# Gathering the keys of AUGRU steps 4 to 11 as 32x32 blocks

## The chip, the core and the metric

The kernel runs on one core of a Trainium2 chip. The time is the device time of one execution in microseconds, the median of several. A core has five engines that run beside each other and wait for one another by semaphores: PE (matrix multiply), DVE (vector), ACT (activations), POOL (here: elementwise work and gathers) and SP (here: issuing DMAs). Data between HBM and the on-chip memory is moved by 16 DMA engines, which serve the queues of SP, ACT and POOL. A gather is an indirect DMA that POOL issues: 128 rows, each from an address that an index gives.

## The reference

1024 users have a history of 100 items with 128 features. The reference runs a GRU over the history, scores each of its states with a small attention network, takes a softmax over the steps, and then runs a second recurrent network, AUGRU, over the same GRU states ("keys"), whose update gate is scaled by an attention weight. A state is picked at each user's own length, and a small network gives one score per user.

```python
    r = sigmoid(i_r + h_r); z = sigmoid(i_z + h_z)       # GRU, 100 steps
    n = tanh(i_n + r * h_n)
    h_new = (1.0 - z) * n + z * h                        # = keys[:, t]
...
attn = softmax(where(mask == 1, score, -inf), axis=1)[..., 0]
pooled = einsum('bt,btd->bd', attn, keys)
att_seq = pooled.T[:T]
...
    r = sigmoid(ti @ aug_Wr.T + aug_br)                  # AUGRU, 100 steps; ti = [h, keys_t]
    u = sigmoid(ti @ aug_Wu.T + aug_bu)
    h_hat = tanh(concatenate([h * r, x_t]) @ aug_Wh.T + aug_bh)
    u = a_t[:, None] * u
    h_new = (1.0 - u) * h + u * h_hat
```

The weight `a_t` of AUGRU step t is row t of the pooled keys, transposed. So AUGRU can't begin its second product before the softmax and the pooling of all 100 steps are done.

## The kernel before, in words

The 1024 users are two halves of 512 columns; a state is a 128 x 512 tile with features in partitions. All numbers are 32-bit floats. The order of the instructions on each engine is the order in which the program writes them (there is no scheduler in between).

**GRU phase** (`gru_phase`, L180). In each of 100 steps, for each half, PE does six 128x512 products (L501; two matmul instructions each in the profile), ACT and DVE the gates, and the attention network of the step before follows (L663). POOL keeps a masked sum of the history and the weighted sum of the keys, `pooled` (L580 to L600). After each step DVE transposes the new state in 32x32 blocks (`transpose`, L540, DVE L550) into a tile `kt` that holds G = 4 steps, and SP writes it to HBM, to `keys_d[q]`, for AUGRU. There are two layouts:

- Groups q below `WHOLE` = 2, that is steps 0 to 3 and 4 to 7, are stored as whole rows: one row per user with four steps of 128 features. Each step of a half costs four DMAs of 64 KB (L556).
- Later groups hold eight steps and are stored as blocks: partition p of `kt` as it stands, in one DMA of 1 MB per half and four steps (`store`, L562, L564).

**The hand-over.** AUGRU takes the users sorted by length, so that later steps are narrower (`WIDTHS`, 512 columns at step 0, 496 at step 4, 96 from step 83 on). Keys are therefore read back by gathers through sorted indices (`load_rows`, L153). A group of whole rows takes 4 gathers per half, of 256 KB each (`gather`, L142 to L144). A group of blocks takes one gather for 32 users, 16 for a half, each of 128 rows of 1 KB (L168); in the AUGRU phase a tiny POOL copy in front of each (L167) reads one column of `rest`, a tile that the current half-step just wrote, so that gathers are spread over the half-steps ("pace").

Rows of group 0 are gathered in the last 30 GRU steps. Those of group 1, half 0, in step T-2, those of half 1 right after the loop (L867, L885). Behind the loop come the last softmax blocks, the rest of the pooling (POOL L589 to L600 for half 0, DVE for half 1), the write of `pooled_d` (L941, L1208) and eight gathers `att_r` of it (`gather_weights`, L987); PE turns them into the weights of steps 0 and 1 (L996).

**AUGRU phase** (`augru_phase`, L943). A half-step (`half_step`, L1069) closes the two gates of step t of one half on PE (L1058: pr, pu), then opens the three gates of the next half-step from its key (`open_gates`, L1049, L1054: pr, ph, pu); the product ph with the reset state follows in the next half-step. ACT does two sigmoids and a tanh; DVE the five products L1082, L1084, L1086, L1092 and L1095, where L1095 writes `rest`, a tile of a pool with three buffers. SP loads the attention weights two steps ahead (L1027).

`load_key` (L1032) makes the key tile two steps ahead, in the half-step of step t - 2. From whole rows that is four PE transposes into a PSUM bank (L1040) and an ACT copy (L1041). From blocks it is one DVE block transpose (L1044), since a 32x32 block needs only to be turned in itself.

Which gathers stand in which half-step is planned by `spread` (L1192): the gathers of group q begin when group q - 1 becomes current and end three or four steps before group q is needed. Gathers go into `kp`, a pool of four buffers; `kx`, a pool of two buffers of half that size, holds `kt` tiles in the GRU phase and the early rows at its end.

Of the kernel before, what the change touches and what calls it, by code (L numbers as in the profile page):

```python
# [9 lines left out]
F32 = mybir.dt.float32  # L10
# [9 lines left out]
P = 128  # L20
B = 1024
T = 100
HB = 512
NH = B // HB
NG = B // P
GH = HB // P

R = 32
KH = HB // R
# [20 lines left out]


G = 4
WHOLE = 2
READ = [G] * WHOLE + [2 * G] * ((T - WHOLE * G) // (2 * G))
READ += [T - sum(READ)] * (sum(READ) < T)
FIRST = [sum(READ[:q]) for q in range(len(READ))]
# [22 lines left out]
def kernel(ctx: ExitStack, tc: tile.TileContext, a: dict, out: bass.AP):  # L79
# [26 lines left out]
    nc = tc.nc  # L106
# [32 lines left out]
    kx = ctx.enter_context(tc.tile_pool(name="kx", bufs=NH))  # L139
    later = {}  # L140
# [10 lines left out]
    rows = {}  # L151

    def load_rows(q, i, width, tiles):  # L153

        n = READ[q]
        if q < WHOLE:
            tag = "kt" if q else "once"
            r = rows[q, i] = tiles.tile([P, GH, n * P], F32, tag=tag, name="rows")
            for g in range(GH):
                gather(r[:, g, :], keys_d[q], g, i)  # L160
                yield
            return
        r = rows[q, i] = tiles.tile([P, KH, n * R], F32, tag="rows", name="rows")
        for k in range(-(-width // R)):
            if later.get("pace") is not None:

                nc.gpsimd.tensor_copy(r[:, k, 0:1], later["pace"])  # L167
            nc.gpsimd.indirect_dma_start(  # L168
                out=r[:, k, :],
                out_offset=None,  # L170
                in_=keys_d[q],
                in_offset=bass.IndirectOffsetOnAxis(ap=idx_k[:, k, i : i + 1], axis=0),
            )
            yield

    def all_of(steps):
        for _ in steps:
            pass

    def gru_phase(pools):  # L180
# [34 lines left out]
        kp = pools.enter_context(tc.tile_pool(name="kp", bufs=3 * NH))  # L215
# [578 lines left out]
        def stage(count=1):  # L794
            for _ in range(count):
                if soft["stages"]:
                    soft["stages"].pop(0)()
# [8 lines left out]

        rest = load_later()
        early = [load_rows(0, i, HB, mid) for i in range(NH)]
        more_early = [load_rows(1, i, HB, kx) for i in range(NH)]

        late, again, early_from = 6, 24, 84
        for s in range(T):
            last = s == T - 1
            n, due = divmod(s - again, 4)
            n, i = divmod(n, NH)
            more_history = 0 <= n < late

            def loads():
                for half in halves:
                    for m in range(1, AHEAD + 1) if s == 0 else (AHEAD,):  # L820
                        if s + m < T:
                            half.load(s + m)
                            if s + m >= late:
                                half.load_mask(s + m)
                    if s == T - AHEAD:
                        half.load_features()
                if more_history and due == 0:
                    halves[i].load(n, again=True)
                    halves[i].load_mask(n)

            def after_gate():
                if s:
                    take(s - 2)
                    for half in halves:
                        half.product(s - 1)
                loads()

            staged = None
            for half in halves:
                half.gru(  # L840
                    s,
                    after_gate if half.i == 0 else nothing,
                    (lambda: half.transpose(s - 1)) if s else nothing,
                )
                if half.i == 0:
                    staged = bool(soft["stages"])
                    stage(0 if last else 1)
            exponents()
            if s == 0:
                attention_weights()  # L850
            else:
                if not staged:
                    next(rest, None)
                if s == 1:
                    item_part()
                attend(s - 1)

            for n_x in range(s + (s > early_from), min(s + (s >= early_from), T - 1) + 1):
                for half in halves:
                    if n_x >= late:  # L860
                        half.history(n_x)
            for half in halves:
                if last:
                    half.cross_features()

            if s == T - 2:
                all_of(more_early[0])  # L867
            for half in halves:
                half.pool(2 if len(half.todo) > 7 or s >= 92 else 1, nc.gpsimd)
                if s >= GATHER:  # L870
                    next(early[half.i], None)
            if more_history and due == 2:
                halves[i].history(n)
# [8 lines left out]
            for f in these:  # L882
                next(features[f])

        all_of(more_early[1])  # L885
        take(T - 2)
        for half in halves:
            half.product(T - 1)
# [12 lines left out]
        n = ENDS[-3] - ENDS[-4] + 1  # L901
# [19 lines left out]
            half.store((T - 1) // G)  # L921
        halves[1].pool(T, nc.vector)
        stage()
        halves[0].pool(T, nc.gpsimd)
        some(5, 6)
        some(7)
# [3 lines left out]
        stage()  # L930
        halves[0].pool(T, nc.gpsimd)
        halves[1].pool(T, nc.vector)


        for half in reversed(halves):
            t = blocked(s_bs[NH * (soft["j"] % 2) + half.i])
# [6 lines left out]
    def augru_phase(pools, widths, alive):  # L943
# [7 lines left out]
        kp = pools.enter_context(tc.tile_pool(name="kp3", bufs=4))  # L951
# [35 lines left out]
        def gather_weights(i):  # L987
            r = wp.tile([P, GH, P], F32, name="att_r", bufs=2)
            for g in range(GH):
                gather(r[:, g, :], pooled_d, g, i)  # L990
            return r
# [40 lines left out]
        def load_key(t, i, n=None):  # L1032

            q = max(j for j, first in enumerate(FIRST) if first <= t)
            w, m, r = widths[t], t - FIRST[q], rows[q, i]
            k = qp.tile([P, HB], F32, name="k3")
            if q < WHOLE:
                p = pa.tile([P, HB], F32, tag="a", name="pk3") if n is None else bank("pk3", n)
                for g in range(-(-w // P)):
                    nc.tensor.transpose(p[:, ts(g, P)], r[:, g, ts(m, P)], ident)  # L1040
                nc.scalar.copy(k[:, :w], p[:, :w])  # L1041
            else:
                w = -(-w // R)
                nc.vector.transpose(  # L1044
                    k.rearrange("p (k r) -> p k r", r=R)[:, :w, :], r[:, :w, ts(m, R)]
                )
            keys[t, i] = k

        def open_gates(t, i, banks=(None,) * 3):  # L1049
# [19 lines left out]
        def half_step(t, i):  # L1069


            w, h = widths[t], h3[i][:, : widths[t]]
            before, after = ((t - 1, 1), (t, 1)) if i == 0 else ((t, 0), (t + 1, 0))
            if before in resets:
                open_state(*before)
            pr = close_gate(t, i, "pr", wr, h)
            pu = close_gate(t, i, "pu", wu, h)
            nc.scalar.activation(pr, pr, AF.Sigmoid, bias=later["br"])
            nc.scalar.activation(pu, pu, AF.Sigmoid, bias=later["bu"])
            state = states.pop(1 - i, None)  # L1080
            if state is not None:
                nc.vector.tensor_mul(state[0], state[0], state[1])  # L1082
            r = wp.tile([P, HB], F32, name="r3")[:, :w]
            nc.vector.tensor_mul(r, h, pr)  # L1084
            if state is not None:
                nc.vector.tensor_sub(state[3], state[0], state[2])  # L1086
            if t == 1 and i == 0:
                store_weights(0, pa.tile([P, HB], F32, tag="a", name="pw"))
                first_state(1, spare)
            elif t == 1:  # L1090
                first_weights(1, spare)
            nc.vector.tensor_mul(pu, pu, att.pop((t, i))[:, :w])  # L1092
            rest = wp.tile([P, HB], F32, name="rest")[:, :w]

            nc.vector.scalar_tensor_tensor(  # L1095
                out=rest, in0=pu, scalar=1.0, in1=h, op0=ALU.subtract, op1=ALU.mult
            )
            later["pace"] = rest[:, 0:1]
            resets[t, i] = r, pu, rest
            if after[0] < T and (*after, "pr") not in opened:  # L1100
                open_gates(*after)
            if t == 1 and i:
                store_weights(1, spare)
            if t + 2 < T:
                load_att(t + 2, i)
            if 1 < t < T - 2:
                load_key(t + 2, i)

        def last_state(i):
# [97 lines left out]
        for to, t in later["att", 0][: G - 1]:  # L1207
            nc.scalar.dma_start(out=to, in_=t)  # L1208
        sorted_rows = [gather_weights(i) for i in range(NH)]
        for i in range(NH):  # L1210
            load_key(2, i, (FREE_BANK, None)[i])
        open_gates(1, 1, EARLY_BANKS)
# [118 lines left out]
```

## Time and profile before

| | us |
|---|---|
| median of 10 runs | 2058.49 (2057.82 to 2060.6) |
| the profiled execution, and its span | 2058.26, 2056.4 |
| GRU loop on PE | 4.1 to 1412.7 |
| hand-over, to the first AUGRU half-step that closes gates | 1412.7 to 1462.5 |
| AUGRU steps 1 to 99 and the last network | 1462.5 to 2056 |

The profile is one execution, recorded instruction by instruction. A line of the order of time gives the start and the length in microseconds, the engine, the line of the kernel, the operation, the tiles (out<-in) with shapes, and in brackets how long the engine had been idle and what ended that. "x4" merges neighbours of one kind. A line of a stretch gives, for a window of time, the busy time of each engine with its number of instructions, the granted clock of PE as a share of full speed, the busy share of the DMA engines and GB/s. A line of a group gives busy time, mean length in ns, and idle time in front. Matmuls are pipelined and their ends are modelled, so PE's starts say more than its lengths.

### The profile page before, as it was taken

Reading aid. Unit: us, or ns where it says so; the run is one execution under the profiler, and the core shown is the slowest. Engines: PE = TensorE matmul, PEld = TensorE weight load, DVE = VectorE, ACT = ScalarE, POOL = GpSimd, SP = SyncE. Lnnn points to the kernel's source line nnn. Section 1 sums busy time; section 2 is a strip of 40 time slices with the busy share of each in tenths; the row PEclk is TensorE's granted clock in tenths of the full one; section 3 lists DMA queues with packets and bytes.
Section 4 is the critical chain, followed back from the end, with each engine's and each line's share of the span. In section 5 each row is a group of like instructions: output and inputs, shape, how many; then the busy total and the mean of one; then the engine's idle time right before and its main releaser. Section 6 shows DMA issues by size and latency. Waiting matters only on the chain. (4 is left out here: it accounts for less than half of the span.)

```text
span 2056.4 us, 26797 instructions
## 1 busy us (share of the span) xinstructions
PE 2027.5 (99%) x8320; PEld 979.4 (48%) x8320; DVE 1748.4 (85%) x3050; ACT 831.3 (40%) x1516; POOL 1305.0 (63%) x1299
## 2 busy tenths in 40 slices
PE   8999999999999999999999999999899999999997
PEld 3343343333333333333333333334444556679997
DVE  6888999998989988989889898999567787888886
ACT  3334343343433343433333333343344444445554
POOL 0333939669796959596896868898645434444332
PEclk9999999999999999999999999999999999999999
DMA  4643333323334333333333323323434333333332
GB/s 118 118 94 89 104 103 97 92 81 98 111 105 105 117 104 118 111 103 102 98 103 99 104 90 102 104 88 104 119 103 112 96 91 99 92 98 100 87 77 36
DMA packets 254132, 204.36 MB, mean 99 GB/s; under 512 B 76006, under 2 KB 217034, under 8 KB 253978
## 3 DMA queue, kind: packets, MB, share of 16 engines
q1 hardware_dynamic: 240266, 170.43, 30.0%
q0 software_dynamic: 12128, 31.91, 5.5%
q8 instruction: 68, 1.11, 0.2%
q14 instruction: 86, 0.70, 0.1%
q10 hardware_dynamic: 1584, 0.20, 0.1%
HBM read 146.43 MB, written 54.40 MB: 98 GB/s over the span
## 5 line engine op out<-in xcount | busy, mean ns | idle before, releaser
L501 PE MATMUL ps<-x,wih 128*128 128x512 f32 x1200 | 592.7, 603 | 4.1 <-DMA x<-in_hist_x 4.1
L501 PE MATMUL ps<-hn,whh 128*128 128x512 f32 x1188 | 574.4, 592 | 0.0
L501 PEld LDWEIGHTS ps<-x,wih 128*128 128x128 f32 x1200 | 220.9, 191 | 327.7 <-issue 257.6
L501 PEld LDWEIGHTS ps<-hn,whh 128*128 128x128 f32 x1188 | 225.7, 190 | 284.1 <-issue 274.6
L487 POOL TENSOR_TENSOR xm<-x,m 128x512 f32<-128x512 f32 x200 | 248.2, 1241 | 135.2 <-DMA m<-mask_d 134.8
L532 ACT ACTIVATE ps<-ps,bih 128x512 f32<-128x512 f32 x200 | 132.4, 662 | 476.1 <-DVE ps L531 476.1
L513 ACT ACTIVATE r<-ps,brz 128x512 f32<-128x512 f32 x200 | 137.5, 687 | 384.6 <-PE ps L501 384.0
L488 POOL TENSOR_TENSOR hist<-hist,xm 128x512 f32<-128x512 f32 x200 | 268.8, 1344 | 15.7
L600 POOL TENSOR_TENSOR pooled<-pooled,kw 128x512 f32<-128x512 f32 x191 | 254.0, 1330 | 15.0
L599 POOL TENSOR_TENSOR kw<-kt,e 128x512 f32<-128x512 f32 x191 | 220.0, 1152 | 64.7 <-DVE e L772 64.6
L168 POOL DMA_INDIRECT rows<-keys_d,idx_k x204 | 199.0, 975 | 82.1 <-POOL rows L167 50.2
L576 DVE TENSOR_TENSOR kq<-hn,item 128x512 f32<-128x512 f32 x200 | 224.4, 1161 | 0.0
L663 PE MATMUL pm<-hn,wk 128*32 128x512 f32 x1200 | 211.6, 596 | 3.2 <-ACT q L242 1.7
L663 PE MATMUL pm<-kq,wkq 128*32 128x512 f32 x1200 | 209.2, 592 | 0.0
L1066 ACT ACTIVATE c<-ph,bh 128x96 f32<-128x96 f32 (+41 forms) x198 | 96.5, 487 | 257.2 <-PE ph L1058 228.9
L663 PE MATMUL pm<-mv,w 128*32 128x512 f32 (+1 forms) x808 | 195.8, 598 | 0.7 <-DVE e L753 0.7
L697 DVE TENSOR_TENSOR f<-pm,q 128x512 f32<-128x512 f32 x200 | 128.4, 684 | 53.5 <-PE pm L663 53.4
L167 POOL COPY rows<-rest 128x1 f32<-128x1 f32 x204 | 38.7, 190 | 202.7 <-DVE rest L1095 198.8
L536 DVE TENSOR_TENSOR d<-hn,ps 128x512 f32<-128x512 f32 x198 | 136.1, 687 | 34.8 <-ACT ps L532 32.5
L1082 DVE TENSOR_TENSOR pu<-pu,c 128x96 f32<-128x96 f32 (+41 forms) x197 | 88.3, 448 | 89.3 <-ACT c L1066 80.8
L537 DVE TENSOR_TENSOR d<-ps,d 128x512 f32<-128x512 f32 x200 | 138.4, 692 | 23.7 <-ACT ps L533 6.9
L531 DVE TENSOR_TENSOR ps<-ps,u 128x512 f32<-128x512 f32 x200 | 140.0, 700 | 21.5 <-PE ps L501 0.5
(180 smaller groups left out, 3019.6 us busy)
## 6 DMA issues: line engine op xcount, KB each, us to landing
x<-in_hist_x SPq DMA_DIRECT2D x212, 256.0 KB
keys_d<-kt SPq DMA_DIRECT2D x46, 1024.0 KB
m<-mask_d SPq DMA_DIRECT2D x200, 128.0 KB
keys_d<-kt SPq DMA_DIRECT2D x64, 64.0 KB
rows<-keys_d,idx_k POOLq DMA_INDIRECT x204
s_b<-mv SPq DMA_DIRECT2D x200, 8.0 KB
at<-att_d SPq DMA_DIRECT2D x34, 48.0 KB
mask_i<-in_mask SPq DMA_DIRECT2D x8, 200.0 KB
```

What stands on the lines that cost most here:

```text
L168: nc.gpsimd.indirect_dma_start(out=r[:, k, :], out_offset=None, in_=keys_d[q], in_offset=bass.IndirectOffsetOnAxis(ap=idx_k[:, k, i : i + ...
L487: nc.gpsimd.tensor_mul(d, x, m)
L488: nc.gpsimd.tensor_add(acc, acc, d)
L501: nc.tensor.matmul(p, lhsT=w[:, g, :], rhs=v, start=(j == 0), stop=(j == len(parts) - 1),)
L513: nc.scalar.activation(r, pr, AF.Sigmoid, bias=brz[:, 0:1])
L531: nc.vector.tensor_add(pi, pi, u)
L536: nc.vector.tensor_sub(d, h, pi)
L537: nc.vector.tensor_mul(d, pz, d)
L576: nc.vector.tensor_mul(kq, h, item[:, self.cols])
L599: eng.tensor_mul(d, k, w)
L600: eng.tensor_add(acc, acc, d)
L663: nc.tensor.matmul(p[i][s, :], lhsT=w[:, s], rhs=v, start=start, stop=stop)
```

## The change

`WHOLE` goes from 2 to 1. Group 0 (steps 0 to 3) stays in whole rows; all others are blocks of eight steps, 4 to 11, 12 to 19 and so on to 92 to 99, where they were 8 to 15 and so on with four steps left at the end. So:

- In GRU steps 4 to 7 the 32 small stores become two of 1 MB.
- Half 0 of the new group 1 is gathered by the end of the GRU phase into two `kx` tiles of 8 blocks each: 4 gathers in step T-2, 4 right after the loop, 3 ahead of POOL's second piece of pooling, 5 behind its last. Half 1 is gathered into a `kp` tile behind the `att_r` gathers: 16 gathers without pace copies.
- Keys 4 to 7 are made by DVE block transposes, no longer by PE and ACT. For half 0, keys 4 to 11 take two transposes each, one per `kx` tile. Key 4 is made in step 3 together with key 5; step 2 makes none.

```diff
-WHOLE = 2
+WHOLE = 1
...
         if q < WHOLE:
-            tag = "kt" if q else "once"
-            r = rows[q, i] = tiles.tile([P, GH, n * P], F32, tag=tag, name="rows")
+            r = rows[q, i] = tiles.tile([P, GH, n * P], F32, tag="once", name="rows")
...
-        r = rows[q, i] = tiles.tile([P, KH, n * R], F32, tag="rows", name="rows")
+
+        parts, tag = (2, "kt") if tiles is kx else (1, "rows")
+        some = [
+            tiles.tile([P, KH // parts, n * R], F32, tag=tag, name="rows") for _ in range(parts)
+        ]
+        rows[q, i] = some
         for k in range(-(-width // R)):
+            part, at = divmod(k, KH // parts)
+            r = some[part]
...
-        more_early = [load_rows(1, i, HB, kx) for i in range(NH)]
+        more_early = load_rows(1, 0, HB, kx)
+
+        def gather_early(n):
+            for _ in range(n):
+                next(more_early)
...
             if s == T - 2:
-                all_of(more_early[0])
+                gather_early(4)
...
-        all_of(more_early[1])
+        gather_early(4)
...
         halves[1].pool(T, nc.vector)
         stage()
+        gather_early(3)
         halves[0].pool(T, nc.gpsimd)
...
         halves[0].pool(T, nc.gpsimd)
         halves[1].pool(T, nc.vector)
+        all_of(more_early)
...
-                w = -(-w // R)
-                nc.vector.transpose(
-                    k.rearrange("p (k r) -> p k r", r=R)[:, :w, :], r[:, :w, ts(m, R)]
-                )
+                w, n = -(-w // R), KH // len(r)
+                for j, part in enumerate(r):
+                    u = min(w - j * n, n)
+                    if u > 0:
+                        nc.vector.transpose(
+                            k.rearrange("p (k r) -> p k r", r=R)[:, j * n : j * n + u, :],
+                            part[:, :u, ts(m, R)],
+                        )
...
-            if 1 < t < T - 2:
+
+            if t == FIRST[1] - 1:
+                load_key(t + 1, i)
+            if FIRST[1] - 2 < t < T - 2:
                 load_key(t + 2, i)
...
         sorted_rows = [gather_weights(i) for i in range(NH)]
+        all_of(load_rows(1, 1, widths[FIRST[1]], kp))
```

More of the change, by code (lines that the diff above doesn't have):

```diff
@@ L162, in load_rows @@
             return
-        r = rows[q, i] = tiles.tile([P, KH, n * R], F32, tag="rows", name="rows")
+        parts, tag = (2, "kt") if tiles is kx else (1, "rows")
[3 more added lines that the diff above has]
+        rows[q, i] = some
         for k in range(-(-width // R)):
+            part, at = divmod(k, KH // parts)
+            r = some[part]
             if later.get("pace") is not None:
-                nc.gpsimd.tensor_copy(r[:, k, 0:1], later["pace"])
+                nc.gpsimd.tensor_copy(r[:, at, 0:1], later["pace"])
             nc.gpsimd.indirect_dma_start(
-                out=r[:, k, :],
+                out=r[:, at, :],
                 out_offset=None,
```

## The prediction

> **What bounds the kernel now.** I read the page first, for the shares, then the order of time engine by engine around the steps the change touches.
>
> ```profile
> PE 2027.5 (99%) x8320; PEld 979.4 (48%) x8320; DVE 1748.4 (85%) x3050; ACT 831.3 (40%) x1516; POOL 1305.0 (63%) x1299
> ```
>
> PE is busy all the way, so a change pays only where it takes work off PE or off the one stretch in which PE waits. That stretch is the hand-over between the phases, 1436 to 1462 us. In the GRU phase PE starts a step every 14.07 us, steps 4 to 7 (58.4 to 114.6 us) included; the one longer step nearby, the eighth, carries the sixteen count matmuls of L317.
>
> The order of time on PE, around the last transposes that the change removes:
>
> ```profile
> 1511.54 0.60 PE L1040 MATMUL pk<-ident,rows 128*128 128x128 f32 x4
> 1511.98 0.99 PE L1058 MATMUL ph<-r,wh 128*128 128x492 f32 x2
> ...
> 1516.90 0.60 PE L1040 MATMUL pk<-ident,rows 128*128 128x128 f32 x4
> 1517.34 0.99 PE L1058 MATMUL ph<-r,wh 128*128 128x492 f32 x2
> 1518.16 0.98 PE L1058 MATMUL pr<-h,wr 128*128 128x486 f32 x2
> ...
> 1522.24 0.98 PE L1058 MATMUL ph<-r,wh 128*128 128x486 f32 x2
> ```
>
> See the starts: four transposes hold PE for 0.44 us (1511.54 to 1511.98). A half-step with them runs 1511.98 to 1517.34, 5.36 us; the next, without, 1517.34 to 1522.24, 4.90 us. No line says that PE was idle, in either. So PE's own work is the bound here and the 0.44 really goes.
>
> The order of time on POOL at the hand-over (in brackets: idle before, and what ended it):
>
> ```profile
> 1415.98 1.26 POOL L144 DMA_INDIRECT rows<-keys_d,idx  x1 [0.15 <-issue]
> 1417.55 0.95 POOL L144 DMA_INDIRECT rows<-keys_d,idx  x1 [0.30 <-issue]
> 1418.81 0.96 POOL L144 DMA_INDIRECT rows<-keys_d,idx  x1 [0.31 <-issue]
> ...
> 1434.61 1.08 POOL L589 TENSOR_TENSOR pooled<-pooled,e 128x512 f32<-128x512 f32 x1 [4.50 <-DVE e L786]
> ...
> 1452.87 0.99 POOL L144 DMA_INDIRECT att_r<-pooled_d,idx  x1 [6.50 <-DMA pooled_d<-s_b]
> ...
> 1461.73 0.95 POOL L144 DMA_INDIRECT att_r<-pooled_d,idx  x1 [0.30 <-issue]
> ```
>
> A gather costs POOL 1.26 us from start to start. POOL has two holes, 4.50 and 6.50 us, each ended by another engine. The eight att_r gathers behind the second hole are on the path: PE's L996 waits for their landing, and every AUGRU step follows.
>
> Stretches of time (columns: PE, PEld, DVE, ACT, POOL busy, granted clock, DMA share, GB/s):
>
> ```profile
> 1448.00:1450.00 2.00, 1.43 (x4) 0.36 (x2) 0.00 (x0) 0.60 (x2) 0.00 (x0) 1.00 0.88 147
> 1450.00:1452.00 2.00, 1.97 (x5) 1.02 (x6) 0.00 (x0) 0.46 (x1) 0.00 (x0) 1.00 0.75 115
> 1460.00:1462.00 2.00, 2.00 (x11) 2.00 (x11) 0.94 (x2) 0.00 (x0) 1.39 (x3) 0.50 0.12 33
> 1472.00:1474.00 2.00, 2.00 (x9) 1.15 (x8) 1.02 (x3) 0.00 (x0) 1.72 (x3) 1.00 0.56 162
> ```
>
> While pooled_d is written (1448 to 1452) the DMA engines are already 0.75 to 0.88 busy. And after PE's wait the clock is 0.50.
>
> DVE, order of time and the groups by shape:
>
> ```profile
> 1483.88 0.69 DVE L1095 SCALAR_TENSOR_TENSOR rest<-pu,h 128x506 f32<-128x506 f32 x1
> 1486.63 0.69 DVE L1082 TENSOR_TENSOR pu<-pu,c 128x506 f32<-128x506 f32 x1 [2.07 <-issue]
> ```
>
> ```profile
> L1044 DVE STREAM_TRANSPOSE k<-rows 128x256 f32<-128x256 f32 x12 | 5.2, 436 | 0.3 <-issue 0.3
> ```
>
> DVE has 2.07 us free in an early half-step; a 256-column block transpose takes 0.436.
>
> **The change, part by part.** The sum is made against the profiled execution's 2058.26 us (span 2056.4, 1.86 around it); the median of the runs is 0.23 higher.
>
> GRU steps 4 to 7. On SP's queue 32 issues of 64 KB go (median 0.488 us each, 15.6 us of SP) and 2 of 1 MB come (0.378 each). SP issues x two steps, 28 us, ahead, and PE's only wait for x is 4.1 us at the start. Cost 0, gain 0: PE's matmuls hide all of it. Were that cover gone, it could only be a gain, since SP and the DMAs do less.
>
> Keys 4 to 7 off PE. 2 halves x 4 steps x 0.44 = 3.5 us less on a PE that is the bound: -3.5. Eight ACT copies of 0.57 go too; ACT is 40% busy, 0.
>
> The same keys onto DVE. Step 2 loads nothing, step 3 loads keys 4 and 5. In half-step (3,0) that is four transposes, at most 4 x 0.436 = 1.74 us. The free time is 2.07 - 0.44 = 1.63 once PE's period shrinks, so at worst the multiply L1082 is 0.1 late. Behind it stand r and h; h was written at 1525.32 for a matmul at 1527.92, so PE has about 1.9 us of slack. Cost 0 (ends 0 and 0.1). Half 0's keys 6 to 11 need two transposes, 0.87 instead of 0.67, in half-steps that leave DVE 0.93 idle: 0.
>
> POOL before the hand-over. Step T-2 and the place after the loop issue four gathers each, as before, of half the bytes: 0. Three go into the first hole: 0.15 + 1.57 + 1.26 + 0.96 = 3.9 of 4.50: 0. Five go into the second: 0.15 + 1.57 + 3 x 1.26 + 0.96, and 0.30 to the next, 6.76 of 6.50: 0.26 late, on the path.
>
> Their transfers. Five gathers move 5 x 131 KB beside the writes of pooled_d that the path waits for. No row shows this meeting. The nearest, 162 GB/s at a share of 0.56, makes 289 GB/s for engines that are full. Lower end: 0, if the writes lose nothing. Upper end: all five come first, 655 KB / 289 = 2.3 us. I take two gathers, 262 KB / 289 = 0.9, because POOL issues one in 1.26 us and the writes are over by 1452; the 0.26 runs beside it and is inside it.
>
> By the Trainium skill ("DMA: Bandwidth & Descriptors", Anatomy of one DMA, SWDGE path) a GpSimd DMA costs about 2.0 us plus bytes over 436 GB/s, so many small ones are the wrong way round. Paid one after the other, five would be 5 x 2.3 = 11.5 us, 5.0 over the hole, and the sum 2060.0, an estimate from that page.
>
> POOL after the hand-over. Half 1's 16 gathers stand behind the last att_r gather: 1462.68 + 0.30 + 16 x 1.26 = 1483.1. Nothing is late by itself: key (4,1) is transposed near 1492. But the paced gathers of group 2 stand behind them, and this adds a wait. Their copies read rest of half-step (1,0), a pool of three buffers, so DVE's rest in (2,1) must wait for the second such copy: 1483.1 + 0.19 + 0.27 + 0.97 + 0.27 + 0.19 = 1485.0, against 1483.88 - 0.44 = 1483.4. DVE stands 1.6 us, with L1082, r and h queued behind it, and the 1.63 us it has free there covers it: 0 (ends 0 and 1.6, without the cover). The later copies are caught up by (3,0).
>
> Group boundaries from step 12 on move by four steps: the first paced group issues 30 gathers at two per half-step, where it was 30 at four. All gathers together are 236 where they were 228 (16 + 204 + 8); POOL is busy 20 to 25 of each 50 us from 1500 on, and no row shows DVE waiting for rows: 0.
>
> Sum: 2058.26 - 3.5 + 0.9 = 2055.7; on the median, 2055.9.
>
> **The rivals.**
> *B, the gain is eaten by the new waits on DVE.* If DVE's free time is not where I put it, (2,1) costs 1.6 and (3,0) 1.74, and the path pays 3.3: 2055.9 + 3.3 = 2059.2, no change. For it: 1.6 against 1.63 is a hair's breadth. Against: PE's 1.9 us of slack stands behind each.
> *C, slower: POOL's gathers push the hand-over.* Place: the eight gathers in the two holes, 8 x 1.26 = 10.1 us. If they delay the pooling multiplies or the att_r gathers instead of filling waits, 2058.5 - 3.5 + 10.1 = 2065.1. It is slower than before from 3.5 us on, measurably from 7.6. For it: the second hole is overfull by 0.26. Against: both holes are ended by others (DVE's weights, pooled_d's landing), and DVE's softmax ran at its usual 0.72 beside the gathers of 1416 to 1421.
> *D, faster than I say: transfers don't collide and the clock stays up.* PE's L1058 pair at 1462.51 took 1.71 us to the next against 0.85 at 1474.63, and four L996 matmuls 1.01 against 0.44, both at 0.50 clock: 1.4 us. Without that, and with 0.3 for 0.9: 2053.9. For it: the 0.50 stretches (1440 to 1444, 1457 to 1464) begin and end in the middle of PE's work. Against: PE's wait gets no shorter.
>
> The skill ("TensorE: Matmul & The Clock Gate", Part 1) halves the clock after an idle window of 3.4 us. By it a longer wait could as well add one such window, 1.7 us, an estimate from the page that would make 2057.6.
>
> **How the numbers follow.** Mine 0.48, B 0.10, C 0.18, D 0.24. 0.2% of 2058.5 is 4.1 us, about what a measurement of this kernel can tell from no change. Mine and B lie within it (0.58), D beyond it on the fast side (0.24), C on the slow side (0.18). The predicted time is mine, 2055.9; its own range is the transfer's 0 to 2.3 and the runs' scatter (0.7 below, 2.1 above), 2054.3 to 2059.4. For 8 in 10 it reaches below D, to 2053.0, and above B by a small part of C, to 2060.5.
>
> **What would show it.** L1040 keeps 32 of its 64 matmuls, and PE has no idle time from 1470 to 1520; the half-steps of t = 2 to 5 start 4.85 to 5.1 us apart. The first att_r gather starts 0.3 to 1.2 us after 1452.87. DVE's L1095 shows an idle time ended by POOL's L167 once, near 1484. I am wrong if L589 at 1434.6 or the att_r gathers move by several us, or if PE waits for r or h in steps 2 to 4.

## The result and the profile after

The changed kernel takes 2076.67 us (median of 8 runs, 2074.95 to 2078.85) beside 2058.86 us of the kernel before (28 runs, 2057.68 to 2060.6): a ratio of 1.0088, with a 95% interval of 1.0079 to 1.0096. It is 18 us slower; the forecast was 2.6 us faster than the median shown. The profiled execution took 2076.41 us, its span is 2074.6.

Where the 18.2 us of span lie is seen from the starts of a few instructions that both kernels have (ACT's tanh L1066 is L1083 now; all of the AUGRU lines move by 13 to 17):

| stretch | before | after | difference |
|---|---|---|---|
| start to the GRU's last input product on PE | 1407.7 | 1408.2 | +0.5 |
| to the first weight gather `att_r` | 45.2 | 46.6 | +1.4 |
| to the tanh of half-step (1,0) | 14.6 | 33.8 | +19.2 |
| to the tanh of (6,0) | 55.8 | 51.4 | -4.4 |
| to the tanh of (31,0) | 216.6 | 216.6 | 0.0 |
| to the end | 316.6 | 318.0 | +1.4 |

PE's busy time is the same to 0.1 us, over a longer span (the page's first part):

```profile
PE 2027.6 (98%) x8288; PEld 977.5 (47%) x8288; DVE 1755.4 (85%) x3066; ACT 826.8 (40%) x1508; POOL 1307.5 (63%) x1291
```

One stretch of some 20 us right behind the weight gathers holds the loss. The order of time on PE there, in the changed kernel (start, length, engine, line, operation, and in brackets the idle time before with what ended it):

```profile
1467.60 1.06 PE L1009 MATMUL spare<-ident,att_r 128*128 128x128 f32 x8
1468.49 1.02 PE L1075 MATMUL ph<-r,wh 128*128 128x510 f32 x2
1485.88 2.07 PE L1075 MATMUL pr<-h,wr 128*128 128x510 f32 x2 [16.37 <-DVE h L1021]
```

PE stands still for 16.37 us: the gates of half-step (1,1) need half 1's first state `h`, which DVE makes (L1020, L1021) from the weight row that PE put into `spare` at 1467.60. In the kernel before the same wait is 0.66 us, and DVE is idle for 0.20 us before it gets that row:

```profile
1468.08 1.12 PE L1058 MATMUL pr<-h,wr 128*128 128x510 f32 x2 [0.66 <-DVE h L1008]
```

```profile
1466.60 0.70 DVE L1007 TENSOR_TENSOR spare<-spare,first_u 128x512 f32<-128x512 f32 x1 [0.20 <-PE spare L996]
```

In the changed kernel, DVE's order of time says when it got that row:

```profile
1470.33 0.69 DVE L1033 COPY att_t<-pw 128x512 f32<-128x512 f32 x1 [3.13 <-PE ph L1075]
1484.40 0.70 DVE L1020 TENSOR_TENSOR spare<-spare,first_u 128x512 f32<-128x512 f32 x1 [13.39 <-remote]
1485.14 0.69 DVE L1021 TENSOR_TENSOR h<-spare,first_h 128x512 f32<-128x512 f32 x1
```

DVE does nothing between 1471.0 and 1484.4, and the view finds no instruction that ended this ("remote"). ACT's order of time shows the same for the tanh, which needs `ph` of 1468.49:

```profile
1467.37 0.66 ACT L1096 ACTIVATE pu<-pu,bu 128x510 f32<-128x510 f32 x1 [0.89 <-issue]
1488.61 0.69 ACT L1083 ACTIVATE c<-ph,bh 128x510 f32<-128x510 f32 x1 [20.58 <-PE pr L1075]
```

(The bracket names `pr`, which PE started at 1485.88: the view takes the last signal of PE before the start, and that of `pr` stands at 1488.63, 0.05 us behind the one of `ph`.) So PE's products stand in the profile at 1467 to 1469.5, and those who wait for them are let go one after the other up to 1488.6. POOL's order of time is the only one that is dense in those microseconds:

```profile
1435.12 1.08 POOL L595 TENSOR_TENSOR pooled<-pooled,e 128x512 f32<-128x512 f32 x1 [0.84 <-DVE last L779]
...
1447.02 0.99 POOL L174 DMA_INDIRECT rows<-keys_d,idx_k  x1
...
1452.10 0.96 POOL L174 DMA_INDIRECT rows<-keys_d,idx_k  x1 [0.30 <-issue]
1454.78 0.95 POOL L144 DMA_INDIRECT att_r<-pooled_d,idx  x1 [1.72 <-PE pk L1053]
...
1464.83 0.95 POOL L174 DMA_INDIRECT rows<-keys_d,idx_k  x1 [0.30 <-issue]
1466.09 0.95 POOL L174 DMA_INDIRECT rows<-keys_d,idx_k  x1 [0.30 <-issue]
```

The first hole in front of the pooling took its three gathers without delay (1435.12 is the loop's 0.5 later than 1434.61). Then come five gathers in the second hole, eight weight gathers, then half 1's 16 gathers of the change, one every 1.26 us, until 1484.7. The stretches of time (PE, PEld, DVE, ACT, POOL busy, granted clock, DMA share, GB/s) add what the standstill costs behind its end:

```profile
1450.00:1452.00 2.00, 1.40 (x4) 0.69 (x5) 0.00 (x0) 1.03 (x2) 1.49 (x2) 1.00 1.16 219
...
1474.00:1478.00 4.00, 0.00 (x0) 0.00 (x0) 0.00 (x0) 0.00 (x0) 3.09 (x4) 0.50 0.79 229
1478.00:1482.00 4.00, 0.00 (x0) 0.00 (x0) 0.00 (x0) 0.00 (x0) 3.09 (x4) 0.50 0.40 115
1486.00:1490.00 4.00, 4.00 (x7) 1.95 (x8) 1.79 (x4) 1.24 (x2) 1.88 (x4) 0.50 0.08 18
```

The clock is 0.50 from 1474 until 1490.9, so that the first products after the standstill take about 2 us instead of 1: from this `pr` to the next `pr` behind `spare` it is 5.2 us (1485.88 to 1491.05) where it was 2.7, 2.5 more. Two more stretches answer what was forecast. PE's half-steps with the removed transposes (ph to ph), and DVE in half-step (3,0):

```profile
1514.25 1.00 PE L1075 MATMUL ph<-r,wh 128*128 128x500 f32 x2
...
1519.24 0.99 PE L1075 MATMUL ph<-r,wh 128*128 128x496 f32 x2
```

```profile
1509.33 1.41 DVE L1060 STREAM_TRANSPOSE k<-rows 128x256 f32<-128x256 f32 x4
1510.99 0.69 DVE L1099 TENSOR_TENSOR pu<-pu,c 128x500 f32<-128x500 f32 x1 [0.24 <-ACT c L1083]
```

A half-step takes 4.99 us there, and PE has no idle time in it; DVE has room left after its four transposes. The gain that was forecast is there, and it is buried.

### The profile page after: what moved, and what is told of

Read it like the earlier page. It is cut to its first block, busy times and chain, and to the rows that moved or that the text cites. A ratio compares the mean times of both kernels' runs of the same rounds, so it can differ in the third digit from the quotient of the medians.

```text
span 2074.6 us, 26686 instructions
## 1 busy us (share of the span) xinstructions
PE 2027.6 (98%) x8288; PEld 977.5 (47%) x8288; DVE 1755.4 (85%) x3066; ACT 826.8 (40%) x1508; POOL 1307.5 (63%) x1291
## 4 chain that ended last, share of the span: by engine, by line
PE 91%; DVE 3%; DMA 2%; issue 1%; another core or an unknown queue 1%; ACT 1%; POOL 0%; SPq 0%; DVEq 0%; ACTq 0%; POOLq 0%
PE ps L507 48%; PE pm L669 16%; PE ph L1075 5%; PE pr L1075 4%; PE pu L1075 4%; PE ph L1071 4%; PE pu L1071 4%; PE pr L1071 4%; DMA rows<-keys_d,idx_k 1%; DVE kq L582 1%; DVE ps L537 0%; DVE f L703 0%; DVE u L527 0%; DVE d L543 0%
## 5 line engine op out<-in xcount | busy, mean ns | idle before, releaser
L174 POOL DMA_INDIRECT rows<-keys_d,idx_k x220 | 214.6, 975 | 86.6 <-POOL rows L173 50.9
L1083 ACT ACTIVATE c<-ph,bh 128x96 f32<-128x96 f32 (+41 forms) x198 | 96.5, 488 | 295.8 <-PE ph L1075 248.2
```

Source lines behind the costliest of these rows:

```text
L174: nc.gpsimd.indirect_dma_start(out=r[:, at, :], out_offset=None, in_=keys_d[q], in_offset=bass.IndirectOffsetOnAxis(ap=idx_k[:, k, i : i + ...
```

## The experiments

Twelve kernels were run, some of them more than once, in five sessions (the recorded expectations say "call"). The kernels of one session share a chip and its runs of the kernel before. The paced kernel (e1, g1) and e4 were timed ten times each, f1 and i1 four times; each other variant's time below is that of one execution. The question: what lets DVE and ACT wait for products that PE has long started? All kernels compute everything; three of them (h1 to h3) move something in addition.

### First session: move the gathers, space them, thin them

The paced version (e1) gives half 1's 16 gathers a pace copy each:

```diff
-        all_of(load_rows(1, 1, widths[FIRST[1]], kp))
...
-        ahead, due = gathers(2), spread(2)
+        def both():
+            yield from load_rows(1, 1, widths[FIRST[1]], kp)
+            yield from gathers(2)
+
+        ahead, due = both(), [4] * 4 + [3] * 11
```

> The changed kernel, with half 1's 16 gathers of steps 4 to 11 no longer issued back to back behind the weight gathers, but four per half-step from (1,0) on, each behind POOL's copy of a fresh rest, as the later groups are; the later group follows at three per half-step. Theory A (an unbroken stream of gathers beside PE's work holds up PE's completion signals) and theory B (the gathers hold them up only at that place, where PE takes half 1's weight rows) both expect the hole of 16.4 us in PE gone, no wait of DVE L1020 or L1033 above 2 us, and a time of 2057.2 us (2076.7 less the hole and its follow-up of 19.5; what is left over the kernel before is 0.5 at the start and 1.4 to 1.9 at the hand-over, less the 3.5 of PE). Theory C (the hole has nothing to do with these gathers, it comes from the later hand-over) expects the hole to stay and 2074 to 2077 us.

Measured: 2051.92 us (10 runs) beside 2055.70, ratio 0.9983 (0.9973 to 0.9992). No standstill:

```profile
1466.79 1.06 PE L1009 MATMUL spare<-ident,att_r 128*128 128x128 f32 x8
1467.69 1.02 PE L1075 MATMUL ph<-r,wh 128*128 128x510 f32 x2
1469.37 1.12 PE L1075 MATMUL pr<-h,wr 128*128 128x510 f32 x2 [0.66 <-DVE h L1021]
```

That speaks against theory C: the hand-over is as late as in the changed kernel (46.5 us from the GRU's last input product to the first weight gather), and PE doesn't stand still. Whether the changed kernel would have stood still beside it isn't known; the same pair side by side comes in the third.

In e2 they stay back to back but behind half-step (1,1); one copy of its `rest` stands in front of the first, `due` is `[0] * 4 + [3] * 11`:

```diff
                 half_step(t, i)
+                if t == 1 and i == 1:
+                    burst = load_rows(1, 1, widths[FIRST[1]], kp)
+                    next(burst)
+                    pace, later["pace"] = later["pace"], None
+                    all_of(burst)
+                    later["pace"] = pace
```

> The same 16 gathers back to back, but behind half-step (1,1): one copy of its rest in front of the first, none between them. Theory A: a hole of 10 to 17 us in PE between steps 2 and 3, 2068 to 2076 us. Theory B: no hole above 2 us, 2057 to 2060 us (PE may wait 1 to 3 us for the last keys of step 4).

Measured: 2051.43 us, no standstill (the last keys of step 4 come late and cost PE 0.89 us). In e3 they stay in place with a copy of a constant column in front of each:

```diff
+        later["pace"] = ident[:, 0:1]
         all_of(load_rows(1, 1, widths[FIRST[1]], kp))
+        later["pace"] = None
```

> The changed kernel with a POOL copy in front of each of the 16 gathers that reads the identity and waits for nothing: place kept, one gather per 1.45 us instead of 1.26. Theory A in its narrow form (only gathers issued with nothing between them hold up PE): the hole is gone, 2057 to 2060 us. Theory B: the hole stays, 16 to 20 us long, 2076 to 2080 us.

Measured: 2052.65 us, no standstill. In e4 the paced kernel gets the five gathers that stood in front of `pooled_d`'s last writes moved behind the weight gathers:

```diff
-        all_of(more_early)
...
         sorted_rows = [gather_weights(i) for i in range(NH)]
+        for k in range(11, KH):
+            part, at = divmod(k, KH // 2)
+            nc.gpsimd.indirect_dma_start(
+                out=rows[1, 0][part][:, at, :],
+                out_offset=None,
+                in_=keys_d[1],
+                in_offset=bass.IndirectOffsetOnAxis(ap=idx_k[:, k, 0:1], axis=0),
+            )
```

> The paced kernel with the last five gathers of half 0, which stood in front of the last stores of the pooled rows, moved behind the eight weight gathers, back to back. The first weight gather starts 1.4 to 1.9 us earlier than in the changed kernel. Theory A: 13 gathers in a row, of which five fall beside PE's first work, hold up PE by less than 3 us: 2055.5 to 2058.5 us. Theory B: each of the five holds it up by about 1.3 us: 2061 to 2063 us. If neither holds and the hand-over was all that the five gathers cost: 2055.5 us.

Measured: ratio 0.9983 (0.9972 to 0.9993), no standstill. From the GRU's last input product to the first weight gather it is 45.24 us, where e1 has 46.50 (the kernel before 45.19, the changed one 46.57). So the five gathers cost the hand-over 1.3 us. It isn't POOL's order: POOL stands idle for 1.72 us between the last of them and the first weight gather. The likely cause is the writes of `pooled_d`, which run beside them; their landing is not recorded. The time as a whole doesn't show it.

Every one of the four was free of the standstill, even those two that theories A and B had said would keep it. Either it takes gathers in an unbroken series and this place together, or it is no property of the program. The changed kernel had not run beside them.

### Second session: the changed kernel again, and doses

> The changed kernel once more, unaltered, beside the kernel before. In the three ways tried (paced, late, with copies between) the hole of 16 us in PE was gone, even where the 16 gathers kept their place or stayed back to back. Theory D (it takes both: an unbroken series of gathers, and PE's completions right behind the weight gathers): the hole is there again, and the time lies 17 to 18.5 us above before. Theory E (the hole is no property of the program, it was there on the chip or in the hour of the first measurement): no hole, 2 to 4 us below before.

Measured: 2080.48 us beside 2060.56, ratio 1.0098 (1.0081 to 1.0115), PE idle 19.28 us. f2 has one copy of a constant in front of the 16 gathers:

```diff
-        all_of(load_rows(1, 1, widths[FIRST[1]], kp))
+        burst = load_rows(1, 1, widths[FIRST[1]], kp)
+        later["pace"] = ident[:, 0:1]
+        next(burst)
+        later["pace"] = None
+        all_of(burst)
```

f3 has it behind the 8th (`for _ in range(8): next(burst)` ahead of the copy). f4 issues eight with that loop and no copy, and gives the other eight to `ahead` as in e1, with `due` as `[2] * 4 + [3] * 11`.

> The changed kernel with one POOL copy that waits for nothing between the last weight gather and the first of the 16; the 16 themselves stay back to back. If the 24 gathers in one unbroken series are what counts (theory D1, length): the hole is gone or under 5 us. If the 16 alone do it at this place (theory D2): the hole stays at 14 to 17 us. Theory E: no hole.

> The changed kernel with one such copy behind the 8th of the 16. By length (D1): 16 in a row, then 8; the PE completions from 1466 on fall into the first part, a hole of about 9 us (from 1469.5 to the copy's place near 1475, and its follow-up), or none if 16 are too few. By place (D2): a hole of 8 to 17 us. Theory E: no hole.

> Eight of the 16 stay behind the weight gathers, back to back; the other eight come paced, two per half-step. Dose: with theory D the hole shrinks with the series, to 4 to 9 us (8 gathers less at 1.26 us take 10 us off); a threshold above 16 in a row would leave none. Theory E: no hole.

Measured: f2 2081.93 us, PE idle 19.08; f3 2079.24 us, 14.44 and 3.00; f4 2070.16 us, 10.51 (9.6 above before, where f1 is 19.9 above).

```profile
1480.27 2.07 PE L1075 MATMUL pr<-h,wr 128*128 128x510 f32 x2 [10.51 <-DVE h L1021]
```

One copy breaks nothing; half the gathers make half the loss. That fits theory D2, the number of gathers at this place.

### Third session: the same kernels on one chip

> The changed kernel as it is, one look, as the measure for the three runs beside it: with theory D a hole of 16 us in PE and 17 to 20 us above before; with a hole that depends on the chip (theory E2) either that or, as in the first four runs, none and 2 to 5 us below before.

> The paced version of the first call once more, on the chip of the run above. Theory D: no hole, 2 to 4 us below before, whatever the changed kernel does beside it. Theory E2: where the changed kernel has its hole, this one has a hole as well (its PE completions up to 1475 us lie beside the same weight gathers).

> The 16 gathers back to back behind half-step (1,1) once more. Theory D in the form 'place': no hole, 1 to 4 us below before. Theory D in the form 'unbroken series, anywhere': a hole of 8 to 17 us between 1475 and 1495 us, 7 to 15 us above before.

> A copy in front of each of the 16 once more, in place. If the copies break what holds PE's completions up: no hole, 2 to 3 us below before. If the place and the number of gathers is all: a hole of 14 to 20 us, and 17 to 20 us above before; then the first call's run without a hole was owed to its chip.

Measured, beside 2059.06 of before: changed 2075.64 (PE idle 12.83 and 3.98), paced 2057.11 (10 runs, ratio 0.9992, 0.9982 to 1.0002; PE idle 0.66, as in the first session), late 2069.21, copies 2068.77. PE's wait for half 1's first state, in the changed kernel and in the paced one:

```profile
1480.95 2.07 PE L1075 MATMUL pr<-h,wr 128*128 128x510 f32 x2 [12.83 <-DVE h L1021]
```

```profile
1470.89 1.12 PE L1075 MATMUL pr<-h,wr 128*128 128x510 f32 x2 [0.66 <-DVE h L1021]
```

Both reach the first weight gather as late (46.5 and 46.4 us after the GRU's last input product), so theory C is out, and it is the 16 gathers. The late series and the copies, without a standstill in the first session, have one here, and each is some ten microseconds above before. ACT's waits between 1470 and 1510 us in the late version (engine, line, waited for: us in total, times, longest), in the first session and here:

```profile
ACT c L1083 <- PE ph L1075: 20.4, 7, 3.8
ACT pr L1095 <- PE pr L1075: 2.0, 7, 1.1
```

```profile
ACT c L1083 <- PE ph L1075: 13.1, 5, 3.3
ACT c L1083 <- remote: 10.6, 1, 10.6
```

The 10.6 us that end with no name ("remote") are new; the instructions are the same. So D2's "place" falls: a series at 1.26 us also does it behind half-step (1,1). And whether it does it at all depends on something that isn't in the program. In g2 the series begins at 1477.8 and the first tanh or sigmoid that starts late is that of 1493.29, due at 1490.5. In the changed kernel the unbroken series begins with the weight gathers at 1454.78 and the first late one was due at 1467.8. Both times it is some 13 us, ten gathers, from the first; in f4 it is 11.6 (1455.99, and a sigmoid due at 1467.6 that starts at 1468.82).

### Fourth and fifth session: POOL's work or the bytes

h1 puts eight gathers that nobody needs behind the weight gathers of the paced kernel, 16 bytes per partition each; h3 does it with 1 KB; h2 moves the same 1 MB with one plain transfer on SP's queue. h4 is the changed kernel with a copy of 128x256 in front of each of the 16.

```diff
+        spill = kp.tile([P, KH, 2 * G * R], F32, tag="rows", name="spill")
+        for k in range(8):
+            nc.gpsimd.indirect_dma_start(
+                out=spill[:, k, :4],                                      # h3: [:, k, :256]
+                out_offset=None,
+                in_=keys_d[1].rearrange("n (a c) -> (n a) c", c=4),       # h3: keys_d[1]
+                in_offset=bass.IndirectOffsetOnAxis(ap=idx_k[:, k, 1:2], axis=0),
+            )
```

> The paced version, and behind the weight gathers eight more gathers back to back that nobody needs, of 16 bytes per partition instead of 1 KB, into a buffer of their own. Theory P (POOL's handling of a gather holds PE's completions up): a hole of 5 to 11 us in PE between 1467 and 1482 us. Theory Q (the bytes or their landing in SBUF do): no hole above 2 us. Beside it the real gathers of half 1 start some 10 us later than in the paced version, which may cost 0 to 3 us at the keys of step 4.

> The paced version, and at the same place one plain transfer on SP's queue of the bytes that eight gathers move (1 MB), which nobody needs. Theory P: no hole; DVE may wait some us for the weight rows queued behind it. Theory Q: a hole of 5 to 11 us.

> As the first of these, with 1 KB per partition: the control. Both theories: a hole of 8 to 12 us, as with the eight of the run f4 (9.6 us above before). No hole at all would say that this chip does not show the effect (theory E2).

> The changed kernel with a POOL copy of 128x256 in front of each of the 16 gathers that waits for nothing, so that they start every 1.6 to 2.2 us instead of 1.26 (hole of 12.8 to 16.4) or 1.44 (holes of 5.2 and 5.8). If the gap between gathers lets the completions through: no hole above 2 us, 1 to 3 us below before. If the number of gathers decides: holes of 8 us and more in sum, 8 to 12 us above before.

Measured: 2054.35, 2056.76, 2056.51 and 2060.14 us beside 2054.87. None shows the standstill, not even the control h3, so the fourth session tells nothing about it (what PE loses in h1 and h3, 2.54 and 3.05 us, is a wait for the late keys of step 4). h2 would have told little anyway: nothing held its transfer back, so it started at 1451.62 among the writes of `pooled_d` and pushed the first weight gather to 1458.78. h4 shows something else. Its 16 gathers end at 1491.6, and then DVE waits as the forecast had said it would, for the second pace copy behind them:

```profile
1493.23 0.69 DVE L1112 SCALAR_TENSOR_TENSOR rest<-pu,h 128x506 f32<-128x506 f32 x1 [7.48 <-POOL rows L173]
```

In e3, where the series ends at 1487.0, this wait is 4.46 us and PE loses 0.57 by it; in h4 it is 7.48 and PE loses 3.60.

The last session ran the changed kernel and h1 once more.

> The changed kernel once more. Where before takes 2055 to 2056 us on this chip (theory E2, the hole depends on the chip): no hole, and 2 to 4 us below before. If the hole belongs to this program on every chip: 16 to 19 us above before there too. Where before takes 2059 us or more: 16 to 19 us above it, the control for the run beside it.

> Eight gathers of 16 bytes per partition, back to back behind the weight gathers, beside the paced ones. On a chip where before takes 2059 us or more: theory P (POOL's handling of a gather holds PE's completions up) a hole of 5 to 11 us between 1467 and 1482 us and 3 to 9 us above before; theory Q (the bytes or their landing do) no hole above 2 us there and at most 3 us above before. On the other kind of chip neither is tested, and it lies within 1 us of before as in its first run.

Measured: the changed kernel 2080.03 us beside 2061.22, ratio 1.0096 (1.0079 to 1.0113), PE idle 14.65 and 2.96; the tiny gathers 2070.64 us, PE idle 9.86. Here is h1's kernel twice, in the order of time on DVE and ACT: first as it ran in the fourth session,

```profile
1467.38 0.70 DVE L1020 TENSOR_TENSOR spare<-spare,first_u 128x512 f32<-128x512 f32 x1 [0.20 <-PE spare L1009]
```

```profile
1468.24 0.69 ACT L1083 ACTIVATE c<-ph,bh 128x510 f32<-128x510 f32 x1 [1.53 <-PE ph L1075]
```

then in the last:

```profile
1477.82 0.70 DVE L1020 TENSOR_TENSOR spare<-spare,first_u 128x512 f32<-128x512 f32 x1 [6.37 <-remote]
```

```profile
1477.86 0.69 ACT L1083 ACTIVATE c<-ph,bh 128x510 f32<-128x510 f32 x1 [9.31 <-remote]
```

This settles two things. Gathers of 16 bytes do it like those of 1 KB (9.86 us here, 10.51 in f4, both with eight): the bytes are not needed, and theory Q falls as far as it speaks of bytes. It doesn't follow that POOL's own work on a gather does it. In h1's trace a tiny gather raises 16 landing signals, as many as a full one, and no run takes these away. And the standstill outlasts POOL's part: here POOL is done with its last tiny gather at 1474.88 and PE's signals come from 1477.75 on, 2.9 us later, beside the recorded landing signals of that gather (1477.72 to 1477.95); in f4 it is 2.9 us, too (1475.79, 1478.68).

The other thing: it is PE's signals that are late, not its products. DVE waits for the weight row, ACT for the product `ph` that PE runs after it. Undisturbed, ACT starts 0.86 us after DVE, the time of that product. Held up, both start within 0.04 us, which no product fits into; both results were ready, and the signals came in a bunch. That is also why PE's own lines show nothing: a reader sees the cause only by laying the waiter's start beside the product's. (The Trainium skill says why one should look there: in "Perfetto Trace Analysis", Summary: the profiler window per engine type, a product's record on PE ends with an estimate, and the way of its signal is not in it. The trace agrees: the record of `ph` in the changed kernel ends at 1469.52, and its signal stands at 1488.58.)

## Why the prediction was wrong

Step by step, by its own terms:

- **Keys 4 to 7 off PE, -3.5: right.** From the tanh of (1,1) to that of (6,0) it is 48.4 us before and 44.9 after, -3.5.
- **The same keys onto DVE, 0: right.** The four transposes of half-step (3,0) take 1.41 us and 0.24 us stay free.
- **GRU steps 4 to 7, 0: right within what can be told.** The loop ends 0.5 us later; two kernels with the same GRU code (e1, g1) end it 2.2 us apart.
- **POOL before the hand-over, and the transfers, +0.9: the mechanism fits, the size was too small.** It measures 1.4, and 1.3 between e1 and e4; the end given was 2.3. While `pooled_d` is written the DMA share reaches 1.16 (1450 to 1452 us), where it was 0.75. The 5.0 us that five gathers would have cost one after the other did not come.
- **"POOL after the hand-over": this step failed.** It said of half 1's 16 gathers "nothing is late by itself" and priced them by POOL's order and by DVE's wait behind them, 0. That wait is real, as e3 and h4 show. But the series of gathers kept PE's signals from DVE and ACT: 16.4 us of standstill in the profiled execution, where 0.7 had been (12.8 to 19.3 in the other three, two of which have a second one of 3.0 and 4.0), and 2.5 us of half clock behind it, 18.2. The table has it as +19.2 (19.24) less the 0.88 us by which half-step (1,1) is shorter then, 18.4. So the sign "PE has no idle time from 1470 to 1520" failed, too.
- **Group boundaries, 0: not told apart.** From step 31 on it is 1.4 us more in that one pair of profiles, but the changed kernel's other three have 316.9 to 319.4 us there, a scatter as large.

Sum on the span: 0.5 + 1.4 + 18.4 - 3.5 + 1.4 = 18.2.

Of the rivals, C had the sign and the engine but not the place: POOL's gathers did the harm, not by pushing the hand-over (1.9 us with the 0.5 of the loop) but by what they do to another engine's signals behind it. B's wait in (2,1) appears in e3 and h4, where PE loses 0.57 and 3.60 us by it, and not in the changed kernel, whose half-steps come later than the gathers; D's clock went the other way. What the working lacked was a row in which PE worked beside a series of more than eight unbroken gathers. The trace of before has none in AUGRU: eight weight gathers, then gathers spaced by pace copies. A step that is moved onto an engine was costed by that engine's time alone, and a behaviour without a row was priced at 0 instead of bounded.

**The better version.** The paced kernel keeps the gain and leaves the standstill out: 0.9983 (0.9973 to 0.9992) in the first session, 0.9992 (0.9982 to 1.0002) in the third, where it can't be told from before. It is faster than the kernel before in one of two sessions, by 0.17%, and 18.5 us faster than the one run of the changed kernel in the third.

## What to carry to other kernels

A copy that only spaces gathers may be doing more than its name says. Before a gather is issued without it, look for a row where such a series runs beside the engine that matters; and when an engine waits for a product that stands in the profile long before, lay the start of two waiters beside each other to see whether the product or its signal was late. When a variant is judged, run the version it is to be compared with in the same session: four kernels of the first would have led to a false theory, had the changed kernel not been run again.

## What the hardware showed that was not expected

**PE's signals are held up by a long series of gathers.** The trace also holds the times at which PE's semaphore was raised. In the changed kernel six signals stand between 1470 and 1488.6, and they fit the six products in their order and the starts of those who wait:

| product of PE | its record ends | its signal | who starts then |
|---|---|---|---|
| `pw` | 1467.76 | 1470.30 | DVE L1033, 1470.33 |
| `spare`, first to fourth | 1467.99 to 1468.66 | 1474.54, 1477.36, 1480.18, 1484.38 | DVE L1020, 1484.40 |
| `ph` | 1469.52 | 1488.58 | ACT L1083, 1488.61 |

In the kernel before the same six stand 0.01 to 0.02 us behind the end of their record. The distances are 6, 4, 4, 6 and 6 times 0.70. Only PE's signals are late: those of DVE, ACT and POOL that are recorded stand, all but one or two, at the end of their instruction. The eight weight gathers alone, in the kernel before, hold nothing up; a series at 1.26 us does so after about ten. The Trainium skill's "SBUF — State Buffer", Who interferes with whom, names DVE as the engine that gets into the way of gathers and says that a transfer never contends with a computing engine. These runs agree as far as the bytes go, and show a way of interfering that the section doesn't have.

**It depends on the session, and the traces can be told apart.** In two sessions nothing of this was seen, and before took 2055.70 and 2054.87 us; in all the others, where before took 2058.5 to 2061.2, there it was. In the eight traces without the effect every raise of PE's semaphore is recorded: 2503 to 2505, for 2501 to 2503 products that raise it. In the twelve others, that of before among them, only 2348 to 2374 of some 2500 are. DVE's, ACT's and POOL's fall short by 6 to 11%, and the landing signals of transfers by more (e1 has 17364, g1, the same kernel, 15003). In the traces of before, of the changed kernel and of i2 nearly all that PE's and DVE's lack is missing behind 1300 us, where the gathers are.

The paced kernel, which has no standstill in either, shows the difference best. From the tanh of (1,0) to that of (31,0) both of its profiles take 268.8 us, and from there to the end it is 311.9 us in the first session and 316.9 in the third. There the half-steps are short and gathers come in most; in the third session single half-steps are longer by up to 1.9 us. The longest, in PE's order of time and in ACT's:

```profile
1957.55 0.53 PE L1075 MATMUL ph<-r,wh 128*128 128x152 f32 x2
...
1958.68 0.41 PE L1071 MATMUL ph<-k,wh 128*128 128x146 f32 x2
1960.20 0.52 PE L1071 MATMUL pu<-k,wu 128*128 128x146 f32 x2 [1.11 <-ACT c L1083]
```

```profile
1959.76 0.39 ACT L1083 ACTIVATE c<-ph,bh 128x152 f32<-128x152 f32 x1 [1.80 <-PE ph L1071]
```

The tanh starts at 1959.76 for a product of 1957.55 that takes 0.5 us; PE's signals stand there at 1958.28, 1959.01 and 1959.73, 0.72 apart, and four more follow within 0.17. The kernel before takes 316.6 us for this stretch, so it seems to pay these 5 us too.

**What stays open.** What differs between the sessions is not known; the fourth and the last name the same chip number and behave differently, so the number does not decide it. Signals come late in the very traces that lack records of signals. So the recording itself is a rival: it may be what holds PE's signals up while many are raised. The times of the changed kernel and of all sessions have recorded spans beside them, and no run tells what an execution without a record would take. The changed kernel was never run in a session without the effect; there it might be near the paced one. Nor is it known what part of a gather reaches PE's signals, POOL's work on it or its landing signals. The paced series, which also comes every 1.44 us from 1473 on, holds up nothing in g1, while copies that wait for nothing, at the same 1.44 us, do in g3. In g3 they follow the weight gathers without a break, in g1 POOL is idle for 5.89 us in between; no run tells whether this break or something else decides it.
